# Four layers on one core: how the experts' weights queue, when the return's gathers are asked for, and the order of the scans' opening

## The chip, the cores and the metric

The kernel runs on one core of one Trainium2 chip. The metric is the device time of one execution in microseconds (us). A core has five engines that run their own instruction streams: PE (matmul), DVE (vector), ACT (activation functions), POOL (further vector work and indirect gathers) and SP, which here only issues DMA transfers. They wait for each other through semaphores. ACT and POOL issue transfers as well.

## The reference

The input x has the shape (2, 128, 56, 56) in float32. Four layers follow one another, each of the form `x = x + layer(groupnorm(x))` with 32 groups: an attention over agent tokens, a 3x3 convolution, a mixture of experts over patches, and a bidirectional state-space scan. The change touches the last two:

```python
def _L2_conv_ref(x, router_w, w1, w2):          # 8 experts, top 2, patches of 2x2
    xp = patches(x)                             # (1568, 512)
    probs = softmax(xp @ router_w)
    topv, topi = top_k(probs, 2)                # gate = topv / sum(topv), 0 elsewhere
    for e in range(E):
        val, g = split(xp @ w1[e], 2)           # w1[e]: 512 x 2048
        out = out + gate[:, e:e+1] * ((val * sigmoid(g)) @ w2[e])   # w2[e]: 1024 x 512
    return unpatch(out)

def _mamba(x, ...):                             # one row of the image is one sequence of 56
    xi, z = split(x @ in_w.T)                   # 256 channels each
    xc = silu(causal_conv4(xi))
    dt, Bm, Cm = split(xc @ xproj_w.T)          # rank 8, 16 states, 16 states
    dt = softplus(dt @ dt_w.T + dt_b)
    h = exp(dt * A) * h + (dt * xc) * B         # for each of 16 states, step by step
    y = sum_s(h * C) + xc * D
    return (y * silu(z)) @ out_w.T

y = concat(mamba_f(rows), mamba_b(rows reversed)) @ fuse_w.T        # then a layernorm over the width
```

## The kernel before

**Experts** (class `PatchExperts`). The 2 x 1568 pairs of a token and an expert are sorted by expert into tiles of 128 slots. The program has room for 32 tiles; at least 25 (`fewest`) and on this input 28 run: 25 in straight code, 3 in the branch of a `Switch`. For tile j, `up_weights` and `down_weights` (L1340, L1346) have SP fetch the expert's w1 (4 MB) and w2 (2 MB) into one of two buffers each, `gather` has POOL fetch the rows by an indirect DMA (L1313, `xr`), `up` transposes them on PE (`xr_ps`, L1368), copies them on DVE (`xs_c`) and multiplies by w1 (`h_ps`, L1379, 128 matmuls), and `down` multiplies by w2 (`o_ps`, L1399) and has ACT send the tile's rows to DRAM (`os`). Tile j's `down` is written after tile j+1's `up`. A scheduler places the instructions of each engine from the program's order; `issue_after(x)` asks that what follows be placed after x on the same engine. `fetches` holds the w1 transfers, and the loop asks that tile j's work come behind an early one of them:

```python
            if j > 0:
                behind.enter_context(net.tc.issue_after(fetches[min(j - 1, 1)]))
            with behind:
                e = expert(j)
                w1, w2 = up_weights(j, e), down_weights(j, e)
                ht = up(j, w1, gather(j))
```

**The return** (`combine`, a generator). For each of 7 blocks of an image, POOL gathers two sets of rows from `os` (`g`), DVE adds them (L1480), PE transposes the sum (`y_ps`, L1483), DVE adds that to x (L1456) and takes the statistics of the next groupnorm. After the blocks the norm itself follows: `gn_mv` (L100), two small matmuls `gn_ps` (L104, L116), `gn_d`, `gn_q` (L109, L110), `gn_rstd` with a square root and a Newton step (L66 to L71), and `norm` (L1610, L1611). The first image's return runs beside the expert tiles: when `ahead` = 20 tiles have been written, every row of image 0 is in tiles already done. `next(beside)` takes one step of it; `turns` says at which of five spots (0 to 3 after each group of 32 matmuls, 4 at the tile's end) of which tile a step is taken, and `spot` orders the step behind PE's last matmul and DVE's last operation of the tile. At tile 20 the first `LEAD` = 5 steps, which only issue gathers, are taken at once. The second image's return, `second`, runs after the last tile, in the opening of the scans.

**Scans.** 14 blocks of 448 positions (8 rows of one image) are scanned in two directions, `f` and `b`. A half-block (one direction) has 16 units: 8 pairs of states times two halves m of the channels. For one unit, ACT makes `dA` (L1898), POOL `dBu = dtu * Bs` (L1909), DVE runs the scan (L1928) and multiplies by C (L1939), or POOL does the latter for some units (L1937), and PE sums over states (`y`, L1950). B and C of a half-block come from PE and ACT as rows `low`, go to DRAM (`far`, L1811) and are read back broadcast over partitions: `Bs` for all 8 pairs (L1816, two DMAs of 896 KB) and `Cs` pair by pair (L1822, two DMAs of 112 KB). `dtu` and `dt` are spread likewise (`send_steps`, L1886). `dBu` has 6 buffers, and `push` works 4 units ahead.

What else a half-block needs (conv, silu, low, dt_ps, softplus, gates) is booked in an `agenda` by unit number, 32 to a block; the first block's stages have negative steps, the opening. In the opening each step is followed by a number of steps of `second`, given in a tuple; what remains of `second` is taken one step to a unit in the main loop. This part is scheduled by hand (`manual_schedule`): every engine runs in the order of the program.

Of the kernel before, what the change touches and what calls it, by code (L numbers as in the profile page):

```python
# [8 lines left out]
F32 = mybir.dt.float32  # L9
AF = mybir.ActivationFunctionType  # L10
# [11 lines left out]
BLK = 448  # L22
# [991 lines left out]
class PatchExperts:  # L1014
# [15 lines left out]
    def route(self, dram, wpool, conv):  # L1030
# [7 lines left out]
        self.xd = dram.tile([toks, 512], F32, name="xd")  # L1038
        self.os = dram.tile([TILES * SLOTS, 512], F32, name="os")
        with tc.tile_pool(name="l2_route", bufs=1) as one, tc.tile_pool(  # L1040
            name="l2_route_ps", bufs=2, space=PSUM
# [280 lines left out]
    def run(self, wpool, work, ps, beside):  # L1322
# [13 lines left out]
        starts, fetches = [], []  # L1336

        def up_weights(j, e):
            w1 = ups[j % 2]
            dma = nc.sync.dma_start(w1, w1s[e].rearrange("o c q f -> (o c) q f"))  # L1340
            fetches.append(dma.ins)
            return w1
# [7 lines left out]

        turns = {2: (1, 3, 4), 3: (0, 1, 2, 3, 4, 4), 4: (0, 1)}

# [55 lines left out]
        for j in range(self.fewest):  # L1408
            behind = ExitStack()
            if 0 < j < 4:  # L1410
                behind.enter_context(net.tc.issue_after(starts[0]))
            if j > 0:
                behind.enter_context(net.tc.issue_after(fetches[min(j - 1, 1)]))
            with behind:
                e = expert(j)
                w1, w2 = up_weights(j, e), down_weights(j, e)
                ht = up(j, w1, gather(j))
            if last is not None:
                down(*last)
            last = (j, ht, w2)  # L1420
            if j == self.ahead:
                for _ in range(LEAD):
                    next(beside)
            spot(j, 4)
# [190 lines left out]
def mamba_pair(net, out, wts, combine, keep, norms):  # L1615
# [9 lines left out]
    H = P // 2  # L1625
# [9 lines left out]
    with ExitStack() as ctx:  # L1635
# [127 lines left out]
        class Half:  # L1763
# [43 lines left out]

            def send_low(self):

                far = self.far = dram.tile([2 * S, BLK], F32, name="far", tag="far")  # L1810
                nc.sync.dma_start(far, self.lo[R:, :])  # L1811
                self.B = work.tile([P, PAIRS, BLK], F32, name="Bs", tag="Bs")
                for s in range(2):
                    half = slice(s * H, (s + 1) * H)
                    src = far[:S, :].rearrange("(j s) t -> s j t", s=2)
                    nc.sync.dma_start(self.B[half], src[s].unsqueeze(0).to_broadcast([H, PAIRS, BLK]))  # L1816

# [156 lines left out]
        for n, blk in enumerate(blocks):  # L1974
# [3 lines left out]
            if n == 0:  # L1978
# [7 lines left out]
                book(at + 9, lambda f=f: f.step(1), tag="c", late=1)  # L1986
                book(at + 9, f.send_low)
                for m in range(2):
# [4 lines left out]
                for i, (h, m) in enumerate(((f, 0), (f, 1), (b, 0), (b, 1))):  # L1993
                    book((1, 4, 5, 13)[i], lambda h=h, m=m: h.gate(m))
                book(at + 17, lambda b=b: b.conv(0, AF.Silu))
                book(at + 17, lambda b=b: b.conv(1, AF.Silu), tag="c")
                book(at + 19, lambda: silu(None, None))
                for m in range(2):
# [66 lines left out]
        with tc.manual_schedule(engines={E.PE, E.Activation, E.DVE, E.Pool, E.SP}):  # L2065
            second = arrive(net, combine, 1, gathered, back_bank, ps_of_norms, keep, norms, LEAD2)
            first = min(agenda)
            for step in range(first, 0):
                run(step)
                for _ in range((LEAD2, 0, 0, 0, 0, 0, 1, 0, 1, 2, 1, 1, 1, 1)[step - first] if step - first < 14 else 0):  # L2070
                    next(second)
                fetch(step + 1)
            opening = False
        with tc.manual_schedule(engines={E.PE, E.Activation, E.DVE, E.Pool, E.SP}):
# [5 lines left out]
            for n, (h, u) in enumerate(units):  # L2080
# [15 lines left out]
                waiting.append((h, u))  # L2096
                next(second, None)

# [126 lines left out]
```

## Time and profile before

| | |
|---|---|
| median of 3 runs | 3023.01 us (3020.32 to 3023.93) |
| the profiled execution | 3025.19 us; span on the core 3023.5 |
| mean granted clock of PE | 0.941 |
| busy: PE, DVE, ACT, POOL | 2685.7, 2192.9, 1855.9, 1451.1 us |
| instructions | 39364 |
| first w1 issued; first `xr_ps` | 1010.72; 1036.59 |
| last `o_ps` ends; first scan starts | about 1663; 1700.97 |
| fifth scan starts | 1730.41 |

The profile is one execution on the chip, taken by the hardware profiler. Times are us from the span's start. A timeline row gives the start, the duration, the engine, the line of the kernel, the operation, output<-input with the shape, and how many such instructions lie together; in brackets stands the engine's idle time before it, and what ended it. PE's clock is granted in parts: 1.00 is full speed.

### The profile page before, as it was taken

Reading aid. Unit: us, or ns where it says so; the run is one execution under the profiler, and the core shown is the slowest. Engines: PE = TensorE matmul, PEld = TensorE weight load, DVE = VectorE, ACT = ScalarE, POOL = GpSimd, SP = SyncE. Lnnn points to the kernel's source line nnn. Section 1 sums busy time; section 2 is a strip of 40 time slices with the busy share of each in tenths; the row PEclk is TensorE's granted clock in tenths of the full one; section 3 lists DMA queues with packets and bytes.
Section 4 is the critical chain, followed back from the end, with each engine's and each line's share of the span. In section 5 each row is a group of like instructions: output and inputs, shape, how many; then the busy total and the mean of one; then the engine's idle time right before and its main releaser. Section 6 shows DMA issues by size and latency. Waiting matters only on the chain. (4 is left out here: it accounts for less than half of the span.)

```text
span 3023.5 us, 39364 instructions
## 1 busy us (share of the span) xinstructions
PE 2685.7 (89%) x14926; PEld 1271.7 (42%) x14926; DVE 2192.9 (73%) x1856; ACT 1855.9 (61%) x2943; POOL 1451.1 (48%) x801
## 2 busy tenths in 40 slices
PE   7999999999999699999999688888888888888874
PEld 3333333333325587878877223333333333233321
DVE  5978999999886400001020589999999999999996
ACT  5778788888761100000010478888888888888884
POOL 3000010001323000000110679999999999999995
PEclk9999999999989699999999789999999999999987
DMA  1000000000002577878885544565555554544560
GB/s 56 1 1 1 1 1 1 1 1 1 1 1 60 213 289 306 320 313 311 324 309 210 142 99 117 123 145 121 131 116 121 121 144 121 131 116 121 122 143 28
DMA packets 157933, 369.31 MB, mean 122 GB/s; under 512 B 25156, under 2 KB 114980, under 8 KB 154132
## 3 DMA queue, kind: packets, MB, share of 16 engines
q1 hardware_dynamic: 135744, 339.30, 37.4%
q0 software_dynamic: 5520, 15.62, 1.7%
q10 hardware_dynamic: 16452, 11.61, 1.2%
q8 instruction: 122, 2.00, 0.3%
q14 instruction: 95, 0.78, 0.1%
HBM read 297.89 MB, written 17.20 MB: 104 GB/s over the span
## 5 line engine op out<-in xcount | busy, mean ns | idle before, releaser
L1909 POOL TENSOR_TENSOR dBu<-dtu,Bs 128x896 f32<-128x896 f32 x448 | 922.3, 2096 | 18.2 <-DMA dtu<-sp_u 10.5
L1928 DVE TENSOR_TENSOR_SCAN h<-dA,dBu 128x896 f32<-128x896 f32 x448 | 882.0, 2009 | 26.8 <-ACT dA L1898 21.1
L620 ACT ACTIVATE ex<-sc 128x896 f32<-128x896 f32 (+1 forms) x700 | 603.1, 917 | 128.8 <-PE sc L617 117.6
L1950 PE MATMUL y<-h,both 128*64 128x448 f32 x1792 | 465.1, 611 | 80.0 <-POOL h L1937 73.1
L627 DVE TENSOR_TENSOR ex_sum<-ex_sum,ex 128x1792 f32<-128x1792 f32 (+1 forms) x238 | 492.7, 2070 | 37.9 <-ACT ex L620 23.8
L1379 PEld LDWEIGHTS h_ps<-xs_c,w 128*128 128x128 f32 x3584 | 407.6, 194 | 26.0 <-ACT ot L1402 17.7
L1379 PE MATMUL h_ps<-xs_c,w 128*128 128x128 f32 x3584 | 412.6, 277 | 5.1 <-DMA w<-in_L_conv_w_dram 4.3
L617 PE MATMUL sc<-q,k 32*128 32x448 f32 (+1 forms) x2800 | 405.5, 590 | 3.3 <-ACT ex L620 2.7
L1939 DVE TENSOR_TENSOR h<-h,c_ps 128x1792 f32<-128x1792 f32 (+1 forms) x168 | 326.6, 1944 | 25.3 <-ACT c_ps L1916 7.7
L635 PE MATMUL av<-ex,va 128*32 128x448 f32 (+1 forms) x2800 | 337.0, 556 | 0.1
L1393 DVE TENSOR_TENSOR ht<-h_ps,sg 128x512 f32<-128x512 f32 x56 | 38.6, 692 | 394.5 <-PE h_ps L1379 319.3
L582 POOL TENSOR_TENSOR a_e<-a_e,a_inv 112x784 f32<-112x784 f32 x14 | 41.6, 2974 | 586.2 <-ACT ex L620 394.5
L1898 ACT ACTIVATE dA<-dt,f_A 128x448 f32<-128x448 f32 x448 | 283.1, 637 | 61.6 <-DVE h L1928 48.1
L1898 ACT ACTIVATE dA<-dt,b_A 128x448 f32<-128x448 f32 x448 | 283.3, 636 | 33.7 <-DVE h L1928 24.5
L1950 PEld LDWEIGHTS y<-h,both 128*64 128x64 f32 x1792 | 118.1, 146 | 352.3 <-issue 209.7
L1313 POOL DMA_INDIRECT xr<-xd,whom x28 | 28.2, 1007 | 495.2 <-PE xr_ps L1368 455.0
L1937 POOL TENSOR_TENSOR h<-h,Cs 128x1792 f32<-128x1792 f32 (+1 forms) x70 | 252.8, 3611 | 11.7 <-issue 8.6
L617 PEld LDWEIGHTS sc<-q,k 32*128 32x128 f32 (+1 forms) x2800 | 138.4, 182 | 232.0 <-issue 133.8
L1391 ACT ACTIVATE sg<-h_ps 128x512 f32<-128x512 f32 x56 | 33.5, 598 | 309.5 <-PE h_ps L1379 302.0
L1399 PE MATMUL o_ps<-w,ht 128*128 128x512 f32 x448 | 201.6, 593 | 1.2 <-DVE ht L1393 1.2
L1402 ACT ACTIVATE ot<-o_ps,share 128x512 f32<-128x512 f32 x28 | 19.3, 689 | 246.2 <-PE o_ps L1399 246.2
L625 DVE TENSOR_TENSOR ex_sum<-ex 128x1792 f32<-128x1792 f32 x56 | 114.5, 2044 | 56.3 <-ACT ex L620 56.2
(347 smaller groups left out, 2993.4 us busy)
## 6 DMA issues: line engine op xcount, KB each, us to landing
w<-in_L_conv_w_dram SPq DMA_DIRECT2D x28, 4096.0 KB, 20.5
w<-in_L_conv_w_dram SPq DMA_DIRECT2D x28, 2048.0 KB, 10.7
Bs<-far SPq DMA_DIRECT2D x56, 896.0 KB, 8.7
Cs<-far SPq DMA_DIRECT2D x448, 112.0 KB, 2.9
dtu<-sp_u SPq DMA_DIRECT2D x108, 224.0 KB, 3.8
dt<-dt SPq DMA_DIRECT2D x108, 224.0 KB, 4.9
os<-ot ACTq DMA_DIRECT2D x28, 256.0 KB, 7.8
xd<-xt SPq DMA_DIRECT2D x14, 224.0 KB, 2.7
```

The costliest lines, as they stand in the source:

```text
L617: nc.tensor.matmul(sc[:size, j, :BLK], self.m.k[rows, at : at + size], self.q[rows, :], start=True, stop=True)
L620: nc.scalar.activation(ex[:size, 2 * g : 2 * g + 2, :], sc[:size, :, :BLK], AF.Exp, scale=scale)
L627: nc.vector.tensor_add(self.total[g][:size], self.total[g][:size], ex[:size])
L635: nc.tensor.matmul(self.av[rows, :BLK], self.m.va[:size, i, rows], self.ex[i][:size, h, :], start=i == 0, stop=i == STEPS - 1,)
L1379: mm = nc.tensor.matmul(h_ps[:, i * SLOTS : (i + 1) * SLOTS], w1[:, q, f0 : f0 + P], xc[:, q, :], start=q == 0, stop=q == 3,)
L1399: mm = nc.tensor.matmul(o_ps, ht[:, i, :], w2[:, i, :], start=i == 0, stop=i == nj - 1)
L1898: nc.scalar.activation(self.dA[u][:, r * BLK : (r + 1) * BLK], self.dt2[:, m, r, :], AF.Exp, scale=self.w.A[:, j, 2 * m + r : 2 * m + r + 1],)
L1909: nc.gpsimd.tensor_tensor(self.dBu[u], self.dtu2[:, m], self.B[:, j, :].unsqueeze(1).to_broadcast(shape), ALU.mult)
L1928: nc.vector.tensor_tensor_scan(hf, af, bf, 0.0, ALU.mult, ALU.add)
L1937: nc.gpsimd.tensor_tensor(h4, h4, self.C[j].unsqueeze(1).to_broadcast(shape), ALU.mult)
L1939: nc.vector.tensor_tensor(h4, h4, self.c_ps[:, :BLK].unsqueeze(1).to_broadcast(shape), ALU.mult)
L1950: nc.tensor.matmul(self.y[r * H : (r + 1) * H, m, :BLK], both, self.hc[j][:, m, r, :], start=False, stop=j == PAIRS - 1)
```

## The change

There are three parts.

- **Experts.** A DRAM tile `sign` is new. Tile 0's w1 is requested first, then a DMA of 16 numbers of tile 0's gathered rows to `sign`; this DMA can only be issued once those rows have landed, and it stands in `fetches`. Tile 1's work comes behind it, and the order of SP's weights becomes w1(0), sign, w1(1), w2(0), w2(1), w1(2), w2(2), and so on; it was w1(0), w2(0), w1(1), w2(1).
- **Return.** `turns` is given anew: the five leading steps are taken at spots of tiles 20, 21 and 22, and the later ones at tiles 22 to 24.
- **Opening.** `send_low` sends a first part of B (2 of 8 pairs, for the first direction only), and `send_b` the rest at a later step. The second image's return takes more of its steps in the opening, and none in the main loop. The two convolutions of direction `b` are written without Silu, and one Silu over both follows.

```diff
--- before.py
+++ after.py
@@ -1037,6 +1037,7 @@
 
         self.xd = dram.tile([toks, 512], F32, name="xd")
         self.os = dram.tile([TILES * SLOTS, 512], F32, name="os")
+        self.sign = dram.tile([1, 16], F32, name="sign")
         with tc.tile_pool(name="l2_route", bufs=1) as one, tc.tile_pool(
             name="l2_route_ps", bufs=2, space=PSUM
         ) as ps:
@@ -1348,7 +1349,7 @@
 
         traced, shaped = [None], [None]
 
-        turns = {2: (1, 3, 4), 3: (0, 1, 2, 3, 4, 4), 4: (0, 1)}
+        turns = {0: (4, 4), 1: (1, 3), 2: (0, 1, 4), 3: (0, 1, 2, 3, 4), 4: (0, 0, 1, 2)}
 
         def spot(j, at):
             if j < self.fewest:
@@ -1410,17 +1411,22 @@
             if 0 < j < 4:
                 behind.enter_context(net.tc.issue_after(starts[0]))
             if j > 0:
-                behind.enter_context(net.tc.issue_after(fetches[min(j - 1, 1)]))
+                behind.enter_context(net.tc.issue_after(fetches[min(j, 2)]))
             with behind:
                 e = expert(j)
-                w1, w2 = up_weights(j, e), down_weights(j, e)
-                ht = up(j, w1, gather(j))
+                w1, w2 = up_weights(j, e), None
+                if j == 1:
+                    last = (*last[:2], down_weights(0, e_first))
+                if j > 0:
+                    w2 = down_weights(j, e)
+                xr = gather(j)
+                if j == 0:
+                    e_first = e
+                    fetches.append(nc.sync.dma_start(self.sign, xr[0:1, 0:16]).ins)
+                ht = up(j, w1, xr)
             if last is not None:
                 down(*last)
             last = (j, ht, w2)
-            if j == self.ahead:
-                for _ in range(LEAD):
-                    next(beside)
             spot(j, 4)
         for _ in beside:
             pass
@@ -1805,15 +1811,20 @@
 
                 return lambda: nc.scalar.copy(self.lo, pm[:LOW, :BLK])
 
-            def send_low(self):
+            def send_low(self, pairs=PAIRS):
 
                 far = self.far = dram.tile([2 * S, BLK], F32, name="far", tag="far")
                 nc.sync.dma_start(far, self.lo[R:, :])
                 self.B = work.tile([P, PAIRS, BLK], F32, name="Bs", tag="Bs")
+                self.send_b(slice(0, pairs))
+
+            def send_b(self, some):
+                src = self.far[:S, :].rearrange("(j s) t -> s j t", s=2)[:, some]
                 for s in range(2):
                     half = slice(s * H, (s + 1) * H)
-                    src = far[:S, :].rearrange("(j s) t -> s j t", s=2)
-                    nc.sync.dma_start(self.B[half], src[s].unsqueeze(0).to_broadcast([H, PAIRS, BLK]))
+                    nc.sync.dma_start(
+                        self.B[half, some], src[s].unsqueeze(0).to_broadcast([H, some.stop - some.start, BLK])
+                    )
 
             def send_c(self, j):
                 self.C[j] = work.tile([P, BLK], F32, name="Cs", tag="Cs", bufs=4)
@@ -1984,7 +1995,8 @@
                 book(at + 7, f.low)
                 book(at + 9, lambda f=f: f.step(0))
                 book(at + 9, lambda f=f: f.step(1), tag="c", late=1)
-                book(at + 9, f.send_low)
+                book(at + 9, lambda f=f: f.send_low(2))
+                book(at + 14, lambda f=f: f.send_b(slice(2, PAIRS)))
                 for m in range(2):
                     book(at + 10 + m, lambda f=f, m=m: f.log(m))
                     book(at + 11 + m, lambda f=f, m=m: f.softplus(m), tag=("mm", "c")[m])
@@ -1992,9 +2004,9 @@
                     book(at + 12 + m, lambda f=f, m=m: f.send_steps(m))
                 for i, (h, m) in enumerate(((f, 0), (f, 1), (b, 0), (b, 1))):
                     book((1, 4, 5, 13)[i], lambda h=h, m=m: h.gate(m))
-                book(at + 17, lambda b=b: b.conv(0, AF.Silu))
-                book(at + 17, lambda b=b: b.conv(1, AF.Silu), tag="c")
-                book(at + 19, lambda: silu(None, None))
+                book(at + 17, lambda b=b: b.conv(0))
+                book(at + 17, lambda b=b: b.conv(1), tag="c")
+                book(at + 19, lambda b=b: silu(b, None))
                 for m in range(2):
                     book(2 + 3 * m, lambda b=b, m=m: b.step(m))
                     book(4 + 3 * m, lambda b=b, m=m: b.log(m))
@@ -2067,8 +2079,8 @@
             first = min(agenda)
             for step in range(first, 0):
                 run(step)
-                for _ in range((LEAD2, 0, 0, 0, 0, 0, 1, 0, 1, 2, 1, 1, 1, 1)[step - first] if step - first < 14 else 0):
-                    next(second)
+                for _ in range((LEAD2, 0, 0, 0, 0, 0, 1, 0, 1, 2, 1, 1, 1, 2, 1, 1, 1)[step - first] if step - first < 17 else 0):
+                    next(second, None)
                 fetch(step + 1)
             opening = False
         with tc.manual_schedule(engines={E.PE, E.Activation, E.DVE, E.Pool, E.SP}):
@@ -2094,7 +2106,6 @@
                 if done:
                     done.pop().close()
                 waiting.append((h, u))
-                next(second, None)
 
                 quota = 0 if u == 3 and n > 3 else 2 if u == 7 and n > 7 else 1
                 for _ in range(quota):
```

With the scheduler's result laid beside that of before: POOL's instructions stand in the same order. On PE, tile 1's transposes and tile 2's follow up(0), then comes up(1), and only then the first tile's `o_ps`; the small matmuls of the second norm stand ahead of `conv_b`. On ACT the opening has two table loads where there were four. On DVE, `gn_mv` to `gn_q` stand ahead of the first scan, L69 and L70 behind it, L71, L1610 and L1611 behind the second. On SP the six `Cs` transfers of the first three pairs follow B's first part, then `dtu`, and the rest of B goes out after that.

## The prediction

> **What bounds the kernel now.** I read the page first, then the stages one at a time: the timelines of PE, SP and POOL around the start of the experts, a table of windows over the same stretch, and the timelines of DVE, ACT and POOL over the opening of the scans (1663 to 1745 us). The page's slices, each 75.6 us wide:
>
> ```profile
> PE   7999999999999699999999688888888888888874
> DVE  5978999999886400001020589999999999999996
> PEclk9999999999989699999999789999999999999987
> ```
>
> Three stages follow one another: attention and convolution on PE and DVE (to 1024 us), experts on PE alone (DVE at 0 to 2 tenths), scans on DVE (9). The change touches the two seams, where nobody is full: slice 14 (PE 6, clock 6) and slices 22 and 23. First seam, timeline of PE:
>
> ```profile
> 1022.88 0.69 PE L1306 MATMUL inv<-fold,table 128*128 128x64 f32 x2 [0.39 <-DVE table L1304]
> 1036.59 1.09 PE L1368 MATMUL xr_ps<-ident,xr 128*128 128x128 f32 x4 [13.02 <-DMA xr<-xd,whom]
> 1038.52 17.46 PE L1379 MATMUL h_ps<-xs_c,w 128*128 128x128 f32 x128 [0.84 <-DVE xs_c L1370]
> ```
>
> PE stands 13.02 us for the rows of tile 0. POOL issued that gather at 1024.09, so it took about 12.4 us. The timeline of SP shows what lay in the DMA queues before it, and the windows (PE, PEld, DVE, ACT, POOL busy, then clock, DMA share, GB/s) that they were full, then empty:
>
> ```profile
> 1010.72 0.37 SPq L1340 DMA_DIRECT2D w<-in_L_conv_w_dram  x1
> 1022.53 0.35 SPq L1340 DMA_DIRECT2D w<-in_L_conv_w_dram  x1
> 1056.01 0.33 SPq L1340 DMA_DIRECT2D w<-in_L_conv_w_dram  x1
> ```
> ```profile
> 1024.00:1036.00 12.00, 0.00 (x0) 0.00 (x0) 0.00 (x0) 0.00 (x0) 4.15 (x4) 0.50 1.04 431
> 1042.00:1044.00 2.00, 2.00 (x11) 2.00 (x11) 0.00 (x0) 0.00 (x0) 0.00 (x0) 0.50 1.05 387
> 1044.00:1046.00 2.00, 2.00 (x18) 2.00 (x17) 0.00 (x0) 0.67 (x1) 0.00 (x0) 0.84 1.04 382
> 1048.00:1056.00 8.00, 8.00 (x74) 8.00 (x73) 0.69 (x1) 0.60 (x1) 0.00 (x0) 1.00 0.00 0
> ```
>
> Second seam, timeline of DVE; between the six scans lies the second image's norm:
>
> ```profile
> 1700.97 2.02 DVE L1928 TENSOR_TENSOR_SCAN h<-dA,dBu 128x896 f32<-128x896 f32 x1 [1.43 <-POOL dBu L1909]
> 1707.35 2.02 DVE L1928 TENSOR_TENSOR_SCAN h<-dA,dBu 128x896 f32<-128x896 f32 x1 [4.12 <-ACT dA L1898]
> 1714.21 3.88 DVE L110 SCALAR_TENSOR_TENSOR gn_q<-gn_d,gn_mv 128x1 f32<-128x1 f32 x1
> 1718.02 2.01 DVE L1928 TENSOR_TENSOR_SCAN h<-dA,dBu 128x896 f32<-128x896 f32 x1
> 1722.28 2.00 DVE L70 SCALAR_TENSOR_TENSOR ir_t<-ir_t,gn_rstd 128x1 f32<-128x1 f32 x1
> 1726.24 2.01 DVE L1928 TENSOR_TENSOR_SCAN h<-dA,dBu 128x896 f32<-128x896 f32 x1
> 1730.41 3.92 DVE L1928 TENSOR_TENSOR_SCAN h<-dA,dBu 128x896 f32<-128x896 f32 x2
> ```
>
> A 128x1 operation takes 2 to 4 us here, and each ends where the POOL operation beside it ends (gn_q at 1718.09, POOL's h at 1718.08). The same operations take 0.15 to 0.22 us where POOL is idle (first image's norm, 1572 to 1579). POOL's own timeline:
>
> ```profile
> 1703.96 10.20 POOL L1909 TENSOR_TENSOR dBu<-dtu,Bs 128x896 f32<-128x896 f32 x5 [3.02 <-DMA dtu<-sp_u]
> 1728.33 2.08 POOL L1909 TENSOR_TENSOR dBu<-dtu,Bs 128x896 f32<-128x896 f32 x1 [2.03 <-DVE h L1928]
> 1732.49 4.14 POOL L1909 TENSOR_TENSOR dBu<-dtu,Bs 128x896 f32<-128x896 f32 x2 [2.08 <-DVE h L1928]
> 1738.47 4.12 POOL L1909 TENSOR_TENSOR dBu<-dtu,Bs 128x896 f32<-128x896 f32 x2 [1.83 <-DVE h L1928]
> ```
>
> POOL is ahead of DVE here and waits for it, so DVE is late.
>
> **Part 1, the weights.** SP's order becomes w1(0), sign (a 64-byte DMA that waits for gather 0), w1(1), w2(0), w2(1), w1(2); before it was w1(0), w2(0), w1(1), w2(1). When gather 0 is issued (1024.09) only w1(0) is ahead: 4 MB, 14.4 us from issue to landing when it had the queues to itself (w1(2), issued 1056.01), so done by about 1025.1. The nearest rows for a gather in quiet queues are those of the second return: issued 1668.15, used 1672.25 (4.1 us); the next two 3.4 and 3.5. So xr(0) lands at 1027.5 to 1028.2 instead of 1036.6: -8.4 to -9.1. Against it: the first o_ps no longer covers the copy xs_c(1) (0.69 us), and only the transposes of tile 2 do; +0.5. The part is **-8.2**.
>
> Behind the waiting sign on SP stand w1(1), w2(0) and w2(1). Sign passes at about 1028.3 and w1(1) is issued at 1028.75 (two issues of about 0.4). Alone it lands at 1043.2; h(0), from 1030.1 for 17.46, needs it at about 1047.6. w2(0) and w2(1) follow with 4 MB, at the 400 GB/s of the windows by 1054, and the first o_ps, now behind all of up(1), comes at 1063. w1(2) is issued when up(0) frees its buffer, 8.4 us earlier than now, behind those 4 MB: landed by about 1067.5, wanted at 1070. No stall then; were w1(1) to take 28.3 us, the longest w1 of the trace, it would be +9.4. Gather 4 on POOL waits for sign too, and is needed three tiles later.
>
> Here a rule of the Trainium skill and a row part. PE works from 1036.59, yet the clock is 0.50 to 1044 and 0.84 in the window after: 8 us of work to full speed. "TensorE: Matmul & The Clock Gate" (Part 1, the table of its two states) gives about 3.4 us of sustained work. By the row h(0) keeps its 17.46 us and this adds nothing; by the rule the half-speed stretch would be 4.6 us shorter and save 2.3 more. I take the row, since the pair of blocks at 1015.3 to 1022.5 didn't lift the clock either, and keep -2.3 as an end.
>
> **Part 2, return's turns.** The first image's gathers start when os(19) has landed, and POOL's instructions, order and waits stay as they were: only PE and DVE steps are ordered by these turns. Tile 23's wait (PE idle 3.55 us at 1542.78 for w1, and a block at lower clock behind it) has the same gathers in the queues beside w1. One group of y_ps (0.46 us in PE's rows) moves from ahead of this wait to behind it, which is +0.5 at most; **0**. If the gathers did move out of w1's way, that tile's excess would go: T(24) came 28.9 us after T(23), where a tile takes 21.8 and its four y_ps add 1.8, so -5.3, with part of tile 22's 2.4: -6.3. Ends +0.5 and -6.3.
>
> **Part 3, the opening.** (a) B's first two pairs go alone (448 of 1792 KB), then six Cs pieces (672 KB) and the steps; the rest follows. In 1678 to 1691 DMA is full, and the fourth gather of the return took 9.2 us (1675.98 to 1685.20); the PE transpose behind it holds up sp_ps (PE idle 7.38, ACT 9.41). With 1120 KB there instead of 1792 I put it 2.2 us earlier; ends 0.3 (Cs keep the queue full) and 5.8 (3.4 us, as in quiet queues). Two extra issues of 0.69 us on SP fall where SP was idle (1676.8 to 1692.7). B's second part lands at about 1706, and dBu(4) starts at about 1707. Scan(0) is after the second dt2 and dtu; the norm's matmuls and the six Cs issues ahead of dtu take some back: -1.
>
> (b) The norm. Up to gn2 it stands ahead of scan(0), beside an idle POOL: four operations of about 0.2 us in DVE's wait there. L69 and L70 come after scan(0), L71 and L1610 after scan(1); POOL is in dBu then, so I price them as now: 1.67 + 2.00 and 2.00 + 1.14. In the place of the first, DVE had 4.12 us of waiting anyway. From scan(0) to scan(4) it took 1730.41 - 1700.97 = 29.4 us; it becomes (2.0+3.7) + (2.0+3.2) + 2.0 + (2.0+1.1) = 16.0, or -13.4.
>
> (c) ACT. b's two convolutions now share one Silu: two table loads instead of four between dA of scan(1) and low. A switch takes 1.31 us here (1.95 from one to the next, less 0.64 for the operation). The page "ScalarE: Activation LUTs" (What ACT_TABLE_LOAD costs) gives 2.66, with a drain: 2.6 saved by the row, 5.3 by the page. I take the row; it is what lets scan(1) follow on DVE at all, and isn't added again. low of b waits for that Silu; nothing on the path reads it for 10 us.
>
> So DVE alone could be 14.4 us earlier at scan(4). But POOL has to follow: its idle from the first dBu to 1742 is 3.02 + 2.03 + 2.08 + 1.83 = 8.96, so at most about 10 with the earlier start. dBu(4) may wait up to 2 for B; conv_b's second half at half clock costs up to 2. I take **-9.5**, ends -4 and -14.4.
>
> From 1744 on POOL (1207 of 1279 us) and DVE (1212) are both 95% busy, in the same order after the change, so the shift carries to the end. Sum: -8.2 + 0 - 9.5 = -17.7. The profiled execution, 3025.19 us (span 3023.5 and 1.7 around it), becomes 3007.5. It stands 2.2 above the median of the runs, 3023.01, so the predicted time is 3005.3.
>
> **The rivals.** *One seam only* (chance 0.20). Either the opening gives little, because Cs fill the queue as B did and POOL, not DVE, sets the pace (for: POOL's 95%; against: its three waits for DVE): -8.2 - 2 gives 3013. Or w1(1) comes late (decided at 18.9 us from issue to landing; for: w1's median is 20.5; against: those shared the queues with gathers and w2) and eats part 1: 3023 - 9.5 + 1 gives 3014. *More than the sum* (0.11): the gathers do leave w1's way or the clock rises by the rule, and the opening gives 12: 3023 - 8.2 - 12 - 6.3 is 2996. For the gathers: tile 23 shows a wait to be had; against: POOL's unchanged order and waits. *The change doesn't do what it says of the gathers* is my main case. *Slower* (0.09): the scans' feeding loses its step. Extra DMAs shift which transfers follow one another on SP, where Cs wait 399 us for POOL's h; if dtu or B come later in each of the 28 half-blocks, POOL, which has 5% to spare, stalls. It decides at 17.7 / 28 = 0.63 us a half-block; at 0.9 it is +25, so 3030. Against: SP's order past the opening is the same, and POOL waited for dtu 7.5 us in six places only. *No change* (0.06): both seams' covers turn into new waits; 3021.
>
> **How the numbers follow.** The main case has 0.54, its own range 2999 to 3011 (part 1 -6 to -10.5, part 3 -5 to -14). The range of 8 in 10 takes in the one-seam cases and half of the case of more: 2994 to 3016. About 0.2% (6 us) is what a measurement of this kernel can tell from none. Faster: 0.54 + 0.20 + 0.11 less 0.02 of the one-seam cases that fall within it, 0.83; same 0.08; slower 0.09.
>
> **What would show it.** Right: PE's idle before the first xr_ps near 4 to 5 us, w1(1) issued at about 1028.7 with no wait before h(1); T(24) still 28 us after T(23); no table load between two dA halves of scans(1) and (2); gn_q 0.2 us, ahead of scan(0); scan(4) some 9 to 13 us nearer to the last o_ps. Wrong: a wait for w in h(1) or h(2); POOL's idle at dBu(4) over 2 us; first gathers of the return no longer tied to os(19); more idle before POOL's dBu after 1744.

## The result, and the profile after

The changed kernel takes 3005.74 us (median of 5 runs, 3005.19 to 3010.50), the kernel before 3023.59 us in the same comparison. The ratio is 0.9945, with a 95% interval of 0.9931 to 0.9960: about 17 us less. The forecast was 3005.3 us.

The profiled execution has a span of 3003.3 us. Its page, the slices of PE, DVE and the granted clock (a slice is 75.1 us):

```profile
PE   7999999999989799999999788888888888888874
DVE  5978999999886400000120589999999999999996
PEclk9999999999999799999999789999899999999997
```

The seams are still there, and smaller in time. First seam, timeline of PE (start, duration, then the work; in brackets the idle time ahead of it):

```profile
1018.49 0.69 PE L1307 MATMUL inv<-fold,table 128*128 128x64 f32 x2 [0.40 <-DVE table L1305]
1023.27 1.09 PE L1369 MATMUL xr_ps<-ident,xr 128*128 128x128 f32 x4 [4.09 <-DMA xr<-xd,whom]
1025.19 16.37 PE L1380 MATMUL h_ps<-xs_c,w 128*128 128x128 f32 x128 [0.84 <-DVE xs_c L1371]
1043.06 14.53 PE L1380 MATMUL h_ps<-xs_c,w 128*128 128x128 f32 x128 [0.62 <-issue]
```

The wait for tile 0's rows fell from 13.02 to 4.09 us, and tile 1's matmuls follow without a wait for weights. On SP the sign stands between the first two w1, and passes when the rows are there:

```profile
1006.31 0.38 SPq L1341 DMA_DIRECT2D w<-in_L_conv_w_dram  x1
1023.15 0.27 SPq L1425 DMA_DIRECT2D sign<-xr  x1
1024.52 0.38 SPq L1341 DMA_DIRECT2D w<-in_L_conv_w_dram  x1
```

The windows (PE, PEld, DVE, ACT, POOL busy, then clock, DMA share, GB/s) show the queues less than half full while the gathers run, and PE at full clock in the window from 1030:

```profile
1020.00:1024.00 4.00, 0.73 (x4) 0.72 (x4) 0.00 (x0) 0.00 (x0) 3.08 (x4) 0.50 0.44 130
1024.00:1030.00 6.00, 5.16 (x28) 4.81 (x27) 0.69 (x1) 0.00 (x0) 1.75 (x2) 0.58 0.96 335
1030.00:1034.00 4.00, 4.00 (x38) 4.00 (x37) 0.00 (x0) 1.88 (x2) 0.00 (x0) 1.00 1.01 424
```

Second seam, timeline of DVE:

```profile
1687.72 0.22 DVE L110 SCALAR_TENSOR_TENSOR gn_q<-gn_d,gn_mv 128x1 f32<-128x1 f32 x1
1689.70 2.02 DVE L1939 TENSOR_TENSOR_SCAN h<-dA,dBu 128x896 f32<-128x896 f32 x1 [0.87 <-ACT dA L1909]
1693.23 2.00 DVE L70 SCALAR_TENSOR_TENSOR ir_t<-ir_t,gn_rstd 128x1 f32<-128x1 f32 x1
1695.15 2.01 DVE L1939 TENSOR_TENSOR_SCAN h<-dA,dBu 128x896 f32<-128x896 f32 x1
1697.30 2.00 DVE L1616 SCALAR_TENSOR_TENSOR norm<-gn_mean,gn_rstd 128x1 f32<-128x1 f32 x1
1699.28 2.01 DVE L1939 TENSOR_TENSOR_SCAN h<-dA,dBu 128x896 f32<-128x896 f32 x1
1705.31 2.02 DVE L1939 TENSOR_TENSOR_SCAN h<-dA,dBu 128x896 f32<-128x896 f32 x1 [4.02 <-POOL h L1948]
1708.45 2.02 DVE L1939 TENSOR_TENSOR_SCAN h<-dA,dBu 128x896 f32<-128x896 f32 x1
```

gn_q takes 0.22 us instead of 3.88, ahead of scan(0). L70 and L1616, which still lie beside POOL's dBu, take 2.00 us each (2.00 and 1.14 before). A new idle time of 4.02 us stands ahead of scan(3).

**Where the time went.** Five marks cut an execution into stretches: the end of `inv`, the transposes of tile 21, the end of the last `o_ps`, scan(0) and scan(6) (the seventh unit). The table gives the differences between them, read from the timelines of PE and DVE, one profile to a kernel, in us:

| kernel | parts of the change | inv to tile 21 | tile 21 to last o_ps | o_ps to scan(0) | scan(0) to scan(6) | o_ps to scan(6) |
|---|---|---|---|---|---|---|
| before | none | 468.2 | 171.3 | 37.9 | 35.4 | 73.3 |
| after | 1, 2, 3 | 458.8 | 172.6 | 39.1 | 26.3 | 65.4 |
| e1_weights | 1 | 458.8 | 171.6 | 38.9 | 35.4 | 74.3 |
| e2_turns | 2 | 466.0 | 173.4 | 40.4 | 35.5 | 75.9 |
| e3_opening | 3 | 465.6 | 170.8 | 37.7 | 26.3 | 64.0 |
| e4_sign_free | 2, 3, no wait | 468.0 | 173.7 | 39.3 | 26.3 | 65.6 |
| e5_norm | norm of 3 | 466.0 | 173.7 | 42.6 | 21.9 | 64.5 |
| e6_silu | Silu of 3 | 467.5 | 171.5 | 39.9 | 35.4 | 75.3 |
| e7_bsplit | B of 3 | 467.7 | 173.8 | 34.9 | 35.9 | 70.8 |
| e8_w1_ahead | 1, 2, 3, w1 first | 458.8 | 171.6 | 38.1 | 25.1 | 63.2 |
| e9_paced | 1, 3, gathers paced | 458.8 | 181.5 | 37.8 | 25.2 | 63.0 |
| e10_norm_all | 1, 2, 3, whole norm first | 458.8 | 173.0 | 39.4 | 25.5 | 64.9 |
| e11_silu_behind_dA | e10, Silu later | 459.4 | 173.4 | 39.9 | 22.5 | 62.4 |
| e12_old_turns | e11 without 2 | 458.9 | 171.9 | 38.5 | 22.5 | 61.0 |

Between the two profiled executions the span fell by 20.2 us: -4.4 up to `inv`, -9.4 to tile 21, +1.3 to the last o_ps, +1.2 to scan(0), -9.1 to scan(6), +0.2 after it (with rounding). The first 4.4 us lie in code that the change doesn't touch: `inv` ends anywhere from 1017.7 to 1023.7 us in these profiles, and the kernel before, at 1023.6, had a clock of 0.95 where the changed one had 1.00 (100 to 200 us). The scans after scan(6) vary as well, from 1284.5 to 1299.0 us. So single profiles are compared stretch by stretch below, and times by their ratios.

### The profile page after: what moved, and what is told of

Same layout as the page of the kernel before. It is cut to its first block, busy times and chain, and to the rows that moved or that the text cites. A ratio compares the mean times of both kernels' runs of the same rounds, so it can differ in the third digit from the quotient of the medians.

```text
span 3003.3 us, 39370 instructions
## 1 busy us (share of the span) xinstructions
PE 2679.8 (89%) x14926; PEld 1271.0 (42%) x14926; DVE 2187.2 (73%) x1856; ACT 1851.7 (62%) x2942; POOL 1450.4 (48%) x801
## 5 line engine op out<-in xcount | busy, mean ns | idle before, releaser
L1939 DVE TENSOR_TENSOR_SCAN h<-dA,dBu 128x896 f32<-128x896 f32 x448 | 881.7, 2008 | 25.9 <-ACT dA L1909 19.1
L1961 PE MATMUL y<-h,both 128*64 128x448 f32 x1792 | 466.0, 611 | 81.8 <-POOL h L1948 74.3
L1394 DVE TENSOR_TENSOR ht<-h_ps,sg 128x512 f32<-128x512 f32 x56 | 38.5, 691 | 398.1 <-PE h_ps L1380 324.0
L1909 ACT ACTIVATE dA<-dt,b_A 128x448 f32<-128x448 f32 x448 | 282.8, 635 | 34.9 <-DVE h L1939 25.5
```

The source lines that it names most:

```text
L1909: nc.scalar.activation(self.dA[u][:, r * BLK : (r + 1) * BLK], self.dt2[:, m, r, :], AF.Exp, scale=self.w.A[:, j, 2 * m + r : 2 * m + r + 1],)
L1939: nc.vector.tensor_tensor_scan(hf, af, bf, 0.0, ALU.mult, ALU.add)
L1961: nc.tensor.matmul(self.y[r * H : (r + 1) * H, m, :BLK], both, self.hc[j][:, m, r, :], start=False, stop=j == PAIRS - 1)
```

## The experiments

**e1_weights, e2_turns, e3_opening: each part alone.** The first takes only the edits of `run` around `sign`, the second only `turns` and the loop over `LEAD`, the third only the edits below `send_low`.

> Only part 1 of the change: the order of the experts' weights and the wait of w1(1) for tile 0's gathered rows. Theory (the parts add up, each at its own seam): from the end of inv to tile 21's transposes it takes 9.4 us less than before, as in the changed kernel, and nothing else moves: time 3014 to 3016. Rival (the earlier start of the experts is given back later, so that the gain of the whole comes from the opening): local gain the same, total gain under 4 us. A second rival (the gain at the start is the clock's, not the gather's): xr_ps(0) still waits over 10 us.

Measured: ratio 0.9983 (0.9972 to 0.9994), about 5 us (medians 3018.05 and 3024.81). The wait for xr is 4.20 us and the first stretch takes 458.8, as in the changed kernel. The time came out 2 to 4 us above what was expected; its interval reaches from 2 to 8 us of gain, so the runs alone don't settle whether some of it is given back. The stretches do not show any giving back: the next one is 171.6, as before.

> Only part 2: the new turns of the return's steps, no leading five at once. Theory (POOL's order and waits are the same): the first g gather still starts when os(19) has landed, tile 23 still waits 3 to 4 us for w1, from tile 21's transposes to the last o_ps 0 to +1.3 us: time within 0.1% of before. Rival (the gathers spread and leave w1's way): the wait for w1 goes and the stretch is 5 to 6 us shorter: 3017.

Measured: 0.9992 (0.9982 to 1.0002), no difference that can be told. w is still waited for, 5.5 us in two places (4.1 the longest). The rival is out.

> Only part 3: B in two parts, the second norm early, one Silu for direction b. Theory: from the last o_ps to the seventh scan it takes 7.9 us less, as in the changed kernel (scan(0) about 1 us later, the six units after it about 9 us shorter), and nothing changes after it: time 3015 to 3016. Rival (POOL, at 95% from 1744 on, sets the end, and DVE's lead is given back within the first block): local gain 8, total gain under 3 us.

Measured: 0.9969 (0.9959 to 0.9978), about 9 us. From the last o_ps to scan(6) it takes 64.0 us. The rival, a lead given back within the block, is out for the time as a whole. The three ratios together make 5 + 2 + 9 = 16 to 17 us, and the whole change makes 17: the parts add up.

**e4_sign_free: the order without the wait.** In the changed kernel

```diff
-                    fetches.append(nc.sync.dma_start(self.sign, xr[0:1, 0:16]).ins)
+                    fetches.append(nc.sync.dma_start(self.sign, net.ident[0:1, 0:16]).ins)
```

> The changed kernel, with the sign copied from the identity matrix instead of tile 0's rows: the same order of weights on SP, but w1(1) and both w2 no longer wait for the gather. Theory (the wait, which keeps other weights out of the queues, makes the gain): xr_ps(0) waits again 12 to 13 us after inv, and the time is 8 to 9 us over the changed kernel's, 3013 to 3015. Rival (it is the order that helps: w2(0) behind w1(1)): 4 MB less lie ahead of the gather only if w1(1) comes late, and the wait stays near 4 us, time 3006.

Measured: 0.9973 (0.9961 to 0.9984) against before, where the change has 0.9945: 8 to 9 us of the gain are gone (0.0028 of 3024). The timeline of PE:

```profile
1031.11 1.09 PE L1369 MATMUL xr_ps<-ident,xr 128*128 128x128 f32 x4 [12.24 <-DMA xr<-xd,whom]
```

It is the wait that gains, by keeping other weights out of the queues while the gather is under way, and not the order of w2 and w1.

**e5_norm, e6_silu, e7_bsplit: the pieces of part 3.** The first has only the tuple of steps and the missing `next(second)` of the main loop, the second only direction b's Silu, the third only `send_b`.

> Only the early norm of part 3: B in one part and four table loads as before. Theory (the norm's small DVE operations locked beside POOL's work are the cost): gn_q takes 0.2 us instead of 3.9 and the seven units' stretch from scan(0) to scan(6) falls from 35.4 to 27 or 28 us, nearly all of the 9.1 that the whole part 3 took off. Rival (ACT's table loads between the dA halves hold the scans): it stays over 32 us.

Measured (one profile each): scan(0) to scan(6) in 21.9 us, below what was expected, but scan(0) 4.7 us later than before; together 64.5. That is the whole gain of part 3 (64.0 to 65.6 with all of it). The timeline of DVE shows both: the small operations are short ahead of scan(0), and scan(0) has to stand behind them. Of the 4.7 us, 2.4 lie between the end of dBu(0) on POOL and scan(0); by the other 2.3, dBu(0) itself ends later than before, in the first part of the opening, which this edit leaves alone.

```profile
1703.01 0.22 DVE L110 SCALAR_TENSOR_TENSOR gn_q<-gn_d,gn_mv 128x1 f32<-128x1 f32 x1
1705.25 0.16 DVE L70 SCALAR_TENSOR_TENSOR ir_t<-ir_t,gn_rstd 128x1 f32<-128x1 f32 x1
1705.33 2.02 DVE L1928 TENSOR_TENSOR_SCAN h<-dA,dBu 128x896 f32<-128x896 f32 x1
```

> Only the shared Silu of direction b in part 3. Theory (DVE is held by the norm, not by ACT): two table loads fewer, 2.6 us of ACT, but scan(0) to scan(6) stays within 1 us of 35.4. Rival (ACT sets the pace): it falls by 2.6 us or more.

Measured: 35.4 us, not changed at all. Two table loads less are worth nothing while DVE waits for the norm. Behind scan(6) this kernel even falls back: scan(0) to scan(10) takes 52.0 us, where it took 48.8 before, since DVE waits longer for ACT's `c_ps`. The timelines of DVE, before and in e6_silu:

```profile
1743.83 2.02 DVE L1939 TENSOR_TENSOR h<-h,c_ps 128x1792 f32<-128x1792 f32 x1 [3.52 <-ACT c_ps L1916]
```
```profile
1743.99 2.02 DVE L1939 TENSOR_TENSOR h<-h,c_ps 128x1792 f32<-128x1792 f32 x1 [6.69 <-ACT c_ps L1916]
```

> Only B in two parts. Theory of the prediction: from the last o_ps to the DVE addition of the return's fourth block 22.2 us becomes 20, and scan(0) comes 1 us sooner. Rival (six Cs pieces take the place of B in the queues, and what is gained for the gathers is lost again to PE's clock and the later dtu): scan(0) no sooner, or up to 1.2 us later, as the changed kernel has it; scan(0) to scan(6) stays 35.4.

Measured: the DVE addition of the fourth block comes 19.1 us after the last o_ps instead of 22.2, and scan(0) at 34.9 instead of 37.9: 3 us sooner, where the rival had it no sooner. scan(0) to scan(6) stays at 35.9. Alone the gain doesn't last: scan(0) to scan(10) takes 51.9 us instead of 48.8, again with a longer wait for `c_ps` (6.09 us). With the norm in front it is hardly seen at scan(6), which the whole part 3 reaches in 63.0 to 65.6 us (after, e3, e4, e8, e9) and the norm alone in 64.5.

**e8_w1_ahead: is tile 23's wait a late start?** In the changed kernel w1(j+1) now goes to SP ahead of w2(j):

```diff
-                if j == 1:
-                    last = (*last[:2], down_weights(0, e_first))
                 if j > 0:
-                    w2 = down_weights(j, e)
+                    with net.tc.issue_after(fetches[-1]):
+                        last = (*last[:2], down_weights(j - 1, e_last))
+                e_last = e
...
```

> The changed kernel, with SP's order turned round for every tile: w1(j+1) ahead of w2(j). Now w1(j+1) is issued 0.57 us behind w2(j), which waits for o_ps(j-2), though its own buffer was freed by h(j-1) about 7 us before. Theory (tile 23 waits because w1(23) starts late, and the gathers of the return only use up its slack): w1 is issued 6 to 7 us earlier, the waits of 1.05 and 4.24 us at tiles 22 and 23 go, from tile 21's transposes to the last o_ps it takes 166 to 168 us instead of 172.6: time 2999 to 3001. Rival (the gathers hold w1's packets whenever it is issued): the wait stays over 3 us. Slower side: w2, now second, lands after h and o_ps waits: over 3008.

Measured: 0.9936 (0.9920 to 0.9952), not to be told from the change. w1 is issued 6 us ahead of w2, and the profile has no wait for w left at tiles 22 and 23 (tile 24's transposes 24.2 us after tile 23's, where it was 30.1). But in tile 22 stands a new idle time, and the stretch is only 1.0 us shorter, where 5 to 7 were expected. The timelines of PE, ACT, DVE and SP, in this order:

```profile
1505.49 9.74 PE L1380 MATMUL h_ps<-xs_c,w 128*128 128x128 f32 x64 [4.18 <-ACT ot L1403]
```
```profile
1504.63 0.69 ACT L1403 ACTIVATE ot<-o_ps,share 128x512 f32<-128x512 f32 x1 [13.57 <-remote]
```
```profile
1504.69 0.69 DVE L1371 COPY xs_c<-xr_ps 128x512 f32<-128x512 f32 x1 [4.99 <-remote]
```
```profile
1504.63 0.38 SPq L1347 DMA_DIRECT2D w<-in_L_conv_w_dram  x1
```

By PE's records the transposes end at 1500.45 and o_ps at 1501.30, but ACT, DVE and SP, which wait for them, all go on at 1504.6 to 1504.7. What held PE's work back in these 3 to 4 us the trace doesn't say. Twelve of the fourteen gathers lie at 1487.6 to 1502.8 here. Whether the gathers have a part in it is not shown. The theory's numbers failed; the rival's, a wait of over 3 us, held, but not for the weights that it named.

**e9_paced: gathers kept apart.** In the changed kernel

```diff
-        turns = {0: (4, 4), 1: (1, 3), 2: (0, 1, 4), 3: (0, 1, 2, 3, 4), 4: (0, 0, 1, 2)}
+        turns = {1: (1, 3), 2: (1, 3), 3: (0, 1, 3), 4: (0, 0, 1, 1, 2, 2, 2, 3, 4)}
+        pace = [None]
...
+            if self.ahead < j < self.fewest:
+                beat = work.tile([1, 1], F32, name="beat", tag="beat")
+                pace[0] = nc.gpsimd.tensor_copy(beat, xc[0:1, 0, 0:1]).ins
```

and `spot` orders its steps behind `pace[0]` too.

> The changed kernel, with the first image's gathers held back by the tiles: a copy of one number on POOL, which waits for the xs_c of tile 21, 22 or 23, stands ahead of the pairs asked for at that tile, and the turns give 2, 2 and 3 pairs to tiles 21, 22 and 23 (8 and 6 gathers in tiles 21 and 22 now). Theory (the first 8 gathers in a row use up the slack that the queues have in each tile, so w1 lands late): the waits of 1.05 and 4.24 us at tiles 22 and 23 fall to under 1 us together, tile 21's transposes to the last o_ps takes 167 to 169 us instead of 172.6: 3001. Rival (3.2 MB of gathers cost their time whenever they run): the wait moves to tiles 23 and 24 and stays at 4 us or more: 3006.

Measured: 0.9976 (0.9961 to 0.9990), about 9 us slower than the change, and the stretch takes 181.5 us. (The profiled execution, 3008.38 us, is the fastest of twelve with a median of 3020.71; the trace shows the stretch, not what made the others slower still.) Up to tile 24 the theory is half right: the waits for w are 1.05 and 2.01 us, 3.1 together instead of 5.3, and none of the 1 us that was expected. Then the stretch loses 9.59 us at tile 25. The norm's end now falls on that tile, and DVE's copy for it stands behind it; the timelines of PE and DVE:

```profile
1583.63 2.69 PE L1384 MATMUL h_ps<-xs_c,w 128*128 128x128 f32 x11 [9.59 <-issue]
```
```profile
1576.76 0.15 DVE L1621 COPY norm<-gn_rstd 128x1 f32<-128x1 f32 x1
1582.84 0.69 DVE L1372 COPY xs_c<-xr_ps 128x512 f32<-128x512 f32 x1 [5.93 <-issue]
```

PE's transposes for the copy end at 1573.2, so the norm accounts for the wait up to 1576.9. For the 5.93 us behind it the row names no engine; tile 25 is the first in the branch of the `Switch`, but what DVE does there the trace doesn't say. So the experiment shows that the spacing of gathers matters for w1's wait, and not that spreading them pays.

**e10_norm_all: the rest of the norm ahead of scan(0).** In the changed kernel

```diff
+                    if n == 0:
+                        after.enter_context(tc.issue_after(net.normed_by))
                     h.scan(u)
```

where `normed_by` is the last copy of the norm (L1617).

> The changed kernel, with scan(0) placed behind the whole second norm on DVE (L69 to L71, L1616, L1617 too). POOL is idle there, waiting for dtu. Theory (the norm's operations are long only beside POOL's work): each takes about 0.2 us; scan(0) comes up to 1 us later, scan(1) and scan(2) 2 to 3 us sooner; scan(3) is held by the dA that ACT makes behind the Silu of direction b, so scan(6) comes 0 to 1.5 us sooner and the time is 3004 to 3006. Rival (the norm's chain itself, not POOL, is slow): L69 to L1616 take over 1 us each and scan(6) comes later.

Measured: 0.9940 (0.9923 to 0.9956). On DVE:

```profile
1688.70 0.16 DVE L70 SCALAR_TENSOR_TENSOR ir_t<-ir_t,gn_rstd 128x1 f32<-128x1 f32 x1
1689.09 0.16 DVE L1616 SCALAR_TENSOR_TENSOR norm<-gn_mean,gn_rstd 128x1 f32<-128x1 f32 x1
1704.05 2.02 DVE L1939 TENSOR_TENSOR_SCAN h<-dA,dBu 128x896 f32<-128x896 f32 x1 [6.50 <-POOL h L1948]
```

2.00 us became 0.16 for the same two operations, now that POOL is idle beside them. Scan(1) and scan(2) come 2.4 and 3.0 us sooner, and scan(3) waits 6.50 us instead of 4.02: it is as the theory has it. Scan(6) comes 0.5 us sooner, which is within the scatter of these profiles.

**e11_silu_behind_dA and e12_old_turns: who holds scan(3)?** In the kernel of e10

```diff
-                book(at + 19, lambda b=b: silu(b, None))
+                book(2, lambda b=b: silu(b, None))
...
-                book(0, b.low)
-                book(2, b.send_low)
+                book(3, b.low)
+                book(4, b.send_low)
```

with the steps of direction b's dt, log and softplus at 4, 5, 6 and 6, 7, 8, and two gates one step later.

> The kernel of e10 (whole norm ahead of scan(0)), with direction b's Silu and its two table loads, low, dt and softplus booked two steps later, so that on ACT the dA of scan(2) and scan(3) stand ahead of the Silu. Theory (scan(3)'s wait of 4.0 us in the changed kernel and 6.5 in e10 is for ACT, whose dA stands behind the Silu and behind low's wait for PE, not for POOL's h as the row has it): scan(3) starts 2 to 3 us after scan(2) ends at the latest, scan(0) to scan(6) falls from 25.5 to 18 to 21 us; POOL, without a pause from dBu(1) on, is then the bound. Time 3 to 5 us under the changed kernel's, if the later softplus of direction b costs nothing. Rival (POOL's h holds the scans): scan(3) still starts where POOL's h ends, over 24 us for the six.

In the changed kernel the timelines of ACT and POOL show that two ends fall together ahead of scan(3), which starts at 1705.31:

```profile
1698.52 1.28 ACT L1972 ACT_TABLE_LOAD   x1
1699.81 0.95 ACT L1972 ACTIVATE xc<-xc 128x896 f32<-128x896 f32 x1
1700.78 1.28 ACT L1975 ACT_TABLE_LOAD   x1
1703.48 0.53 ACT L1812 COPY low<-low_ps 40x448 f32<-40x448 f32 x1 [1.42 <-PE low_ps L1809]
1703.91 1.30 ACT L1909 ACTIVATE dA<-dt,f_A 128x448 f32<-128x448 f32 x2
```
```profile
1701.29 3.95 POOL L1948 TENSOR_TENSOR h<-h,Cs 128x1792 f32<-128x1792 f32 x1
```

Measured: 0.9944 (0.9931 to 0.9958), the time of the change and not the 3 to 5 us less that were expected. Scan(3) follows scan(2) at once, while POOL's h starts only later; the timelines of DVE and of POOL:

```profile
1702.52 3.94 DVE L1939 TENSOR_TENSOR_SCAN h<-dA,dBu 128x896 f32<-128x896 f32 x2 [1.37 <-ACT dA L1909]
1738.74 5.93 DVE L1939 TENSOR_TENSOR_SCAN h<-dA,dBu 128x896 f32<-128x896 f32 x3 [9.72 <-ACT dA L1909]
```
```profile
1707.20 3.96 POOL L1948 TENSOR_TENSOR h<-h,Cs 128x1792 f32<-128x1792 f32 x1
```

So it was ACT's dA behind the Silu that held scan(3); the row of the changed kernel named POOL's h because that ended at the same moment, 0.03 us behind dA. Scan(0) to scan(6) took 22.5 us instead of 26.3; the expected 18 to 21 were not reached. The second row of DVE shows one reason for the missing gain: direction b's softplus now comes later on ACT, dA of scan(9) stands behind it, and DVE waits 9.72 us. Scan(0) to scan(10) takes 44.3 us, where the changed kernel took 40.7. Part of that belongs to this one execution, the slowest of its six (3019.91 us; median 3007.73). e12_old_turns has the same opening, and there the wait is shorter:

```profile
1727.78 5.93 DVE L1942 TENSOR_TENSOR_SCAN h<-dA,dBu 128x896 f32<-128x896 f32 x3 [6.57 <-ACT dA L1912]
```

In e12 scan(0) to scan(10) takes 40.8 us, the change's own time. So the gain up to scan(6) was turned into a new wait, by no more than its size; the further 3.2 us of e11 go with a lower clock of PE, which makes `gate_ps` and `sp_ps` there (0.50 over 1721 to 1731; 1.00 for the same work in e12, 1713 to 1723).

> The kernel of e11 with the return's turns of before (part 2 undone). Theory (part 2 costs about 2 us: 172.6, 173.4, 173.7 and 173.0 us from tile 21's transposes to the last o_ps with it, 171.3, 171.6, 170.8 and 171.5 without): that stretch is back at 171 to 172 us and the time 1 to 2 us under e11's. Rival (those differences are chance): 173 us again.

Measured: 0.9944 (0.9931 to 0.9957), and 171.9 us in the stretch. The expectation counted only a part of the runs: e5_norm and e7_bsplit, which have the old turns, had taken 173.7 and 173.8. With the new turns the stretch took 172.6 to 173.7 (five profiles with SP's order of the change or of before), with the old ones 170.8 to 173.8 (seven). A cost of part 2 is not shown.

No kernel of these beats the change by more than the intervals.

## Why the prediction was right, and where its steps were off

**Part 1 (-8.2 us).** Right in mechanism and size. With part 1 the first stretch takes 458.8 to 459.4 us, without the wait 465.6 to 468.2 (mean of seven 467.0): -8.1. The gather took 3.6 us from issue (1019.70) to the transposes (1023.27), where 3.4 to 4.1 was said; w1(1) was issued 4.8 us after the gather, 4.7 was said; h(1) and h(2) had no wait for weights. Three terms moved. Over the seven profiles of each kind, PE's wait for xr is 12.4 us on average without the sign's wait and 4.1 with it: -8.2, where 8.4 to 9.1 was said. The lost cover of xs_c(1) is 0.62, where 0.5 was said. And h(0) takes 16.8 and 16.4 us on average, where it was left at its 17.46. That the last makes good what the first lacks is luck.

The length of h(0) is the place where row and rule parted. PE works from 1023.27; the clock turns full at 1029.0 (0.50 ahead of it and 1.00 behind it give the mean of 0.58 over 1024 to 1030), after 5.7 us of work. That is neither the 8 us of the row nor the 3.4 of the Trainium skill's rule ("TensorE: Matmul & The Clock Gate", Part 1). Over the fourteen profiles it comes 4.9 us (e3_opening, 1030.69 to 1035.54) to 8.1 us (before, 1036.59 to 1044.64) after the first transposes, or 2.9 to 6.1 us after the first matmul of h(0). In the clock records of these traces every stretch at one clock lasts a multiple of 3.41 us, and in thirteen of the fourteen the clock turns full at the end of the first such 3.41 us that h(0) fills (in before 1041.23 to 1044.64, in after 1025.60 to 1029.01); in e3_opening PE was busy for 86% of it. So the row gave the time of one execution, and where h(0) falls between these marks is chance. What share of busy time would be enough is not shown: 3.41 us at 88%, with smaller matmuls, did not lift the clock (after, from 1015.36).

**Part 2 (0).** Right. The first gather is issued 8.9 us after os(19) was sent, as it was before (8.8), and tile 23 still waits for w; the timelines of POOL, ACT and PE:

```profile
1487.75 1.00 POOL L1314 DMA_INDIRECT g<-os,at_i  x1 [7.91 <-DMA w<-in_L_conv_w_dram]
```
```profile
1478.90 0.33 ACTq L1404 DMA_DIRECT2D os<-ot  x1
```
```profile
1529.67 5.44 PE L1380 MATMUL h_ps<-xs_c,w 128*128 128x128 f32 x32 [4.24 <-DMA w<-in_L_conv_w_dram]
```

POOL's row names w; when os(19) landed this trace doesn't hold. In e9_paced it does, 8.1 us after it was sent and 1.0 us ahead of the first gather. The bound of -6.3 "if the gathers did move out of w1's way" was too hopeful: pacing them took 2.2 us off the waits.

**Part 3 (-9.5 us).** With the whole of it, the last o_ps to scan(6) takes 64.0, 65.4 and 65.6 us (e3, after, e4), without any of it 73.3, 74.3 and 75.9: -9.5 of the means (with e8 and e9, which keep part 3 whole, -10.3). At scan(4), where the prediction counted, it is 57.9 us after and 67.4 before: -9.5. But the terms of that sum were mis-sized, and one named the wrong engine.

- Term (a), scan(0) 1 us sooner: single profiles scatter by more than that. Scan(0) comes 37.9 to 40.4 us after the last o_ps without part 3 (before, e1, e2, e6) and 37.7 to 39.3 with it (after, e3, e4, e8, e9), 0.9 sooner by the means. Its two halves show more clearly. B's split was worth more than the 2.2 said: POOL ends dBu(0) 34.9 to 37.3 us after the last o_ps in the nine profiles with the split and 37.9 to 40.4 in the five without, -3.3 by the means. And 2.0 us of it are taken back; the timelines of POOL, ACT and DVE after the change:

```profile
1685.57 2.08 POOL L1920 TENSOR_TENSOR dBu<-dtu,Bs 128x896 f32<-128x896 f32 x1
```
```profile
1688.87 0.20 ACT L67 ACTIVATE ir_t<-ir_v 128x1 f32<-128x1 f32 x1 [0.83 <-DVE ir_v L66]
1688.98 0.62 ACT L1909 ACTIVATE dA<-dt,f_A 128x448 f32<-128x448 f32 x1
```
```profile
1688.68 0.16 DVE L66 TENSOR_SCALAR ir_v<-gn_ps 128x1 f32<-128x1 f32 x1 [0.74 <-PE gn_ps L116]
```

  dBu(0) is ready at 1687.66, but scan(0) starts at 1689.70: the second half of dA(0) stands on ACT behind ir_t, and ir_t stands behind the chain from gn_mv over PE to gn_mean, gn_q, PE again and ir_v. Before, scan(0) started 0.03 us behind dBu(0). The prediction named "the norm's matmuls and the six Cs issues". The matmuls are two links of this chain; the Cs issues don't show, since e7, which has them ahead of dtu, has the earliest dBu(0).
- Term (b), the norm: -13.4 to scan(4) by DVE alone, -10.7 measured (29.4 to 18.7). L69 and L70 took 1.55 and 2.00 (1.67 and 2.00 said), L71 and L1616 0.18 and 2.00 (2.00 and 1.14 said). What was missing is the 4.02 us ahead of scan(3).
- The limit: "POOL has to follow" gave at most about 10. The limiter that the runs show at scan(3) is ACT, with the Silu, its tables and `low` ahead of dA. So the cap of about 10 was near the mark for another reason than the one given, and that the sum came out as well as it did is luck in part. Term (c) saw those loads as a gain (two fewer), not as the next wait.
- Term (c), that fewer loads let "scan(1) follow on DVE at all": wrong. In e5_norm, with all four loads, scan(1) has no wait for ACT; in e6_silu, with two, it still has one of 2.79 us (4.12 before).

**The carry to the end.** The ratio of the whole, 0.9945, agrees with the sum of parts, so no later stretch took the gain back by more than the interval. The profiles show it too: scan(100), in the fourth block, comes 340.3 us after the last o_ps with part 3 whole (mean of after, e3, e4, e8, e9) and 350.4 without any of it (before, e1, e2). The rival of a disturbed feeding of the scans is out by this.

## What to carry to other kernels

A small latency-bound transfer that the next stage waits for should be let through before bulk transfers are queued: here one 64-byte transfer that depends on it, placed in the queue of the bulk, held that back until the rows had landed (w1(1) was issued 5.3 us after the end of `inv`, where it had been 1.0 us ahead of it) and saved 8. Short operations of a serial chain belong where the engine that shares their access is idle; here the same operations cost 0.2 us or up to 2 us each. And when a wait is removed, look for the next engine whose instruction stands in order behind something slow: moving the Silu once more only moved the wait to scan(9).

## What the runs showed of the hardware

- A 128x1 operation of DVE with its inputs in SBUF takes 0.16 us with POOL idle (e10) and up to 2.00 us beside POOL's dBu (after), ending within 0.03 us of the POOL operation; L71 took 0.18, since the dBu beside it had only 0.17 us to go (1697.08 to 1697.25). The scans, one of whose inputs is in PSUM, took 2.0 us either way. The Trainium skill's page "SBUF — State Buffer" (Who interferes with whom) has this rule: a DVE instruction with two SBUF inputs contends with a POOL instruction that reads SBUF, one with at most one, outside its 2-port modes, doesn't. The trace agrees, and the size here is the rest of POOL's running operation.
- A gather of 128 rows took 3.5 us with quiet queues and about 12 us beside the weights, though it is issued on POOL and they on SP (e1 and e4: xr_ps 4.20 and 12.24 us after inv).
- The releaser in a row can be one that ended at the same moment by chance (POOL h for scan(3), which ended 0.03 us behind ACT's dA), and a wait of four engines for PE's records of 3 us earlier (e8) has no named cause.
